# Queries and keys of two head groups projected at once, and spread to padded tiles by transfers

## The chip, the cores and the metric

The kernel runs on one core of one Trainium2 chip. The metric is the device time of one execution in microseconds; the median of three runs of the kernel before is 4207.95 us (4204.61 to 4209.77).

## The reference, cut to what matters

Two layers of a "macaron" block follow each other: a mixture of experts, an attention and a mixture of experts again; then a recurrence, an attention with rotary and relative positions and causal mask, and the recurrence again. Tokens: two sequences of 2048, 256 features, float32. The change concerns the two attentions, 16 heads of 16 features each.

```python
# layer 0                                # layer 1
q = x @ Wq.T * (1 / sqrt(D))             q = shape(x @ w_q.T)
k = x @ Wk.T                             k = shape(x @ w_k.T)
v = x @ Wv.T                             v = shape(x @ w_v.T)
                                         q = _apply_rotary_interleave(q, cos, sin) / 4
                                         k = _apply_rotary_interleave(k, cos, sin)
scores = einsum(q, k)                    scores = einsum(q, k) + einsum(q, rel)
attn = softmax(scores)                   attn = softmax(where(causal, scores, -1e18))
out = (attn @ v) @ Wff.T + bff           out = (attn @ v + einsum(attn, rel)) @ w_o.T
x = x + out                              x = x + out
```

`x` in these lines is the layer-normalised input of the attention; `rel` is an embedding of the clipped distance of query and key.

## The kernel before, in words

The features of the normalised input lie on the partitions (`xnT`, two halves of 128), 512 tokens at a time. The 16 heads are treated in four groups `g` of four heads `j`. A head has only 16 features, but TensorE's row tiles have 32 partitions; so the weights of queries and keys are laid out by `heads` (L1390) with 16 columns of weights and 16 of zeros for each head, and one projection (`mm2`, L135, line L138: two matmuls over the two halves of the features) gives 128 rows: four heads at partitions 0, 32, 64 and 96, each with 16 rows of data and 16 of padding. Row 16 of each padded head has a job: in the keys it holds 1 (added from `krow`, L53, as a bias), and in the queries it takes minus the largest score of each query (`subtract`, L573), so that the score matmul itself subtracts the maximum before the exponential.

**Attention 0** (`attention0`, L641) goes over 32 groups `t` = (sequence `b`, block of 512 queries `qc`, head group `g`). Steps are numbered, eight to a group (`PER`). A step has two halves `n`; in each half TensorE computes four score tiles for the exponentials of an earlier group (`exponential`, L691: 128 keys by 512 queries for each of four heads) and four for the maxima of the present group (`largest`, L678), then the side jobs due at this step, and then the weighted sums of the half-step before (`weighted`, L701). ScalarE turns scores into exponentials (L699), VectorE takes maxima (L686), ScalarE copies the weighted sums out of PSUM (L590), and GpSimd adds them up (L592). Side jobs are put into a table `jobs` with the step at which they are due (`at`): `keys` (L658, ScalarE adds `krow` as it copies, L663), `vals`, `queries` (L670, one for each group, due at step PER*t - 1, copied by ScalarE at L675), `subtract`, `divide`, `outputs_T`, `outputs`. Before the first step, at step -1, eight key projections of the first sequence are made; eight more follow in steps 3 to 6. `pT`, the exponentials, has 12 buffers; keys have 5, queries 3.

**Attention 1** (`attention1`, L898) is causal, so groups with different `qc` have different numbers of key blocks. Its 32 groups are in the order: `qc` 1 for all `g`; then `qc` 2 and `qc` 0 in turn for each `g`; then `qc` 3. A planner (L1153 to L1169) gives each group the steps of its maxima (`Ms` to `Me`), of its exponentials (`Es` to `Ee`), of its positions (`Rs`) and the earliest step `By` of its relative scores; `early` (L1179) is the step of its query projection. `rotate` (L927) makes queries and keys: projection (L931), copy by ScalarE (L933), a shuffle that swaps neighbouring partitions by VectorE (L935), two multiplications with the tables of cosines and sines, the bias for keys and an addition (L937 to L941) by GpSimd, or by VectorE before step 0. `by_position` (L962) multiplies queries with the relative embedding, writes the result through DRAM in a skewed layout and reads it back as `band` (L977, L984); `largest` adds the band, and stores it for `positions_load` (L1053, L1130). The tiles named "s2" serve `rotate`, `by_position`, `positions_load` and `positions_T`; there are four buffers for all. Two tables hold the buffers of queries (4) and keys (12).

TensorE, ScalarE and VectorE issue their instructions in the order in which the program writes them (`manual_schedule`, L1308). The order on GpSimd and on SP, which issues the transfers, is set by the compiling framework's scheduler. An instruction waits at the head of its queue until its operands and its output buffer are free; the ones behind it wait with it. The weights of a later stage take the memory of an earlier one, and their loads wait for its last reader.

Of the kernel before, what the change touches and what calls it, by code (L numbers as in the profile page):

```python
# [10 lines left out]
F32 = mybir.dt.float32  # L11
# [21 lines left out]
G = 4  # L33
# [9 lines left out]
def macaron_kernel(ctx: ExitStack, tc: tile.TileContext, t: dict, out: bass.AP):  # L43
# [9 lines left out]
    krow = const.tile([P, 1], F32, name="krow")  # L53


# [6 lines left out]
    nc.sync.dma_start(out=krow, in_=t["krow"])  # L62
# [69 lines left out]
    def rows(j):  # L132
        return slice(32 * j, 32 * j + 32)

# [376 lines left out]

    HV = H // 2
    VW = DH + 1

    class Pieces:
# [3 lines left out]
        def __init__(self, s, name, norm, weights_o, bias):  # L519
# [4 lines left out]
            for n in range(2):  # L524
                m = self.keep.tile([P, CPB, J, 32], F32, name=f"mneg{n}")
                nc.gpsimd.memset(m, 0.0)
                self.mnegs.append(m)
            self.cn, self.cT, self.o, self.pTs, self.q = ({} for _ in range(5))

# [111 lines left out]
    def attention0(norm, tail, wq, wk_, wv, wo, bff):  # L641
# [7 lines left out]
        with ExitStack() as s:  # L649
            z = Pieces(s, "a0", norm, wo, bff)  # L650
# [6 lines left out]

            def keys(b, g, qc):  # L658
                if qc == 0:
                    kT[b, g] = kpool.tile([P, S], F32, name="kT", bufs=5)  # L660
                pk = bank()
                mm2(pk, wk_[:, :, g], slice(None), z.xnT(b, qc))
                nc.scalar.activation(kT[b, g][:, ts(qc, TB)], pk, AF.Identity, bias=krow)  # L663
# [6 lines left out]
            def queries(t):  # L670
                b, qc, g = groups[t]
                pq = bank()
                mm2(pq, wq[:, :, g], slice(None), z.xnT(b, qc))
                q[t] = wk.tile([P, TB], F32, name="q", bufs=3)
                nc.scalar.activation(q[t], pq, AF.Copy, scale=1.0 / 16.0)  # L675
                mx[t] = wk.tile([P, CPB * J, SB], F32, name="mx")
# [14 lines left out]
            def exponential(t, kb, j):  # L691
# [6 lines left out]
                z.pTs[t, kb, j] = wk.tile([P, TB], F32, name="pT", bufs=12)  # L698
# [18 lines left out]
            for b in range(B):  # L717
# [9 lines left out]
                for g in range(G):  # L727
                    for qc in range(SB):
                        due = first - 6 + PER * g + qc
                        at(due if b else (-1 if g < 2 else 2 * g - 1 + qc // 2), keys, b, g, qc)  # L730
# [4 lines left out]
            for t, (b, qc, g) in enumerate(groups):  # L735
                at(PER * t - 1, queries, t)
# [161 lines left out]
    def attention1(norm, tail, w, relk, relv, kbias, dramp, skew):  # L898
# [4 lines left out]
        with ExitStack() as s:  # L903
            z = Pieces(s, "a1", norm, w["o"], None)
            wk, q = z.wk, z.q
            groups = []
            for b in range(B):
                groups += [(b, 1, g) for g in range(G)]
                groups += [(b, qc, g) for g in range(G) for qc in (2, 0)]
# [17 lines left out]
            def rotate(dst, wa, b, qc, bias):  # L927
# [3 lines left out]
                mm2(pa, wa, slice(None), z.xnT(b, qc))  # L931
# [5 lines left out]
                e.tensor_tensor(dst, xa, cos[b, qc], ALU.mult)  # L937
# [3 lines left out]
                e.tensor_tensor(dst, dst, xb, ALU.add)  # L941

            def keys(b, qc, g):
                if qc:
                    kT[b, qc, g] = wk.tile([P, TB], F32, name="kT", bufs=12)
                elif g % 2 == 0:
                    pair = features_slot()
                    for i in range(2):
                        kT[b, qc, g + i] = pair[:, i, :]
                rotate(kT[b, qc, g], w["k"][:, :, g], b, qc, kbias)  # L950
# [5 lines left out]
            def queries(t):  # L956
                b, qc, g = groups[t]
                q[t] = wk.tile([P, TB], F32, name="q", bufs=4)
                rotate(q[t], w["q"][:, :, g], b, qc, None)
                mx[t] = wk.tile([P, CPB, J, MX], F32, name="mx")  # L960
# [193 lines left out]
            for n, (b, qc, g) in enumerate(groups):  # L1154
# [4 lines left out]
                if n > 3:  # L1159
                    start = max(start, Ee[n - 4] + 2)  # L1160
# [10 lines left out]
            for n, (b, qc, g) in enumerate(groups):  # L1171
# [7 lines left out]
            early = [  # L1179
                max(Ms[n] - 6, Ee[n - 4] + 1) if n > 3 else Ms[n] - 6 for n in range(NG)  # L1180
            ]
            for n in range(NG):
                at(Me[n] + 1, z.subtract, n)
            for n in range(NG):
                at(early[n], queries, n)
            for b in range(B):
                for qc in range(SB):
# [3 lines left out]
                    free = early[index[b, done_, G - 1]] if done_ is not None else f - 12  # L1191
# [273 lines left out]
```

## Time and profile before

| what | value |
|---|---|
| median of three runs | 4207.95 us |
| the profiled execution | 4206.7 us |
| its span | 4204.5 us |
| TensorE busy | 4101.3 us (98%) |
| VectorE, ScalarE, GpSimd busy | 65%, 60%, 43% |
| attention 0, from the first key projection to the last output (L624) | 356 to 2133 us |
| attention 1, from its first query projection to its last output (L624) | 2663 to 4014 us |
| TensorE clock granted, mean | 0.988 of full speed |

In the profile's lines, times are microseconds and means of one instruction nanoseconds. PE is TensorE (PEld its weight loads), DVE VectorE, ACT ScalarE, POOL GpSimd, SPq SyncE's queue, from which transfers start. `s<-b,a_q 128*128 128x512` is a matmul into the PSUM tile `s` with weights of 128 by 128 and a moving tile of 128 partitions by 512 columns. A float32 matmul appears as two records. After a bar come busy time and mean, and after another the idle time ahead of the group with what ended it.

### The profile page before, as it was taken

To read this page: it belongs to the slowest core of one execution; us is meant where nothing else is said; L and a number is where in the kernel's file an instruction comes from. 1 tells how busy PE (TensorE), PEld (TensorE's weight loads), DVE (VectorE), ACT (ScalarE), POOL (GpSimd) and SP (SyncE) were. 2 spreads that over 40 slices of the span, in tenths; PEclk is the share of its full clock that TensorE was granted. 3 is DMA by queue.
4 is the path that set the end of the run, shared out by engine and by line. 5 is a ranking of instruction groups with operands and counts; after the bars stand their busy time and mean duration, and the time that the engine had idled before them with its cause. 6 is when DMAs were issued, how large, how long until landed. Compare 5 with 4: busy or idle time off the path is not lost.

```text
span 4204.5 us, 77295 instructions
## 1 busy us (share of the span) xinstructions
PE 4101.3 (98%) x28512; PEld 1966.6 (47%) x28512; DVE 2720.4 (65%) x6190; ACT 2542.8 (60%) x5155; POOL 1804.3 (43%) x1651
## 2 busy tenths in 40 slices
PE   7999999999999999999989989999999999999999
PEld 4664433333344333333346645555554455554445
DVE  6245787888766778787743444667677665667533
ACT  2332788888877788888833322365657665666832
POOL 4244233336333333333442340466646865654410
PEclk9999999999999999999999999999999999999999
DMA  7341000000000000000043420235432333431201
GB/s 252 119 126 51 1 1 1 1 1 1 1 1 2 1 1 1 1 1 1 9 151 121 128 76 0 71 84 116 100 65 66 74 81 81 107 86 39 46 22 41
DMA packets 355513, 224.29 MB, mean 53 GB/s; under 512 B 146624, under 2 KB 338496, under 8 KB 355136
## 3 DMA queue, kind: packets, MB, share of 16 engines
q1 hardware_dynamic: 342848, 185.77, 17.2%
q0 software_dynamic: 12288, 33.57, 2.5%
q8 instruction: 227, 3.72, 0.4%
q14 instruction: 150, 1.23, 0.1%
HBM read 114.17 MB, written 105.12 MB: 52 GB/s over the span
## 4 chain that ended last, share of the span: by engine, by line
PE 90%; DVE 4%; POOL 3%; issue 1%; DMA 1%; ACT 1%; SPq 0%; POOLq 0%; ACTq 0%; DVEq 0%
PE s L694 13%; PE s L138 12%; PE s L706 12%; PE s L682 10%; PE s L1121 6%; PE s L368 6%; PE s L1007 6%; PE s L1092 6%; PE s L387 3%; PE s L624 1%; PE s L559 1%; PE s L1102 1%; PE s L1106 1%; PE s L1085 1%; PE s L850 1%
## 5 line engine op out<-in xcount | busy, mean ns | idle before, releaser
L592 POOL TENSOR_TENSOR o<-o,part 128x512 f32<-128x512 f32 (+3 forms) x800 | 964.5, 1206 | 1354.2 <-ACT part L590 1350.4
L686 DVE TENSOR_REDUCE mx<-s 128x1 f32<-128x512 f32 x2048 | 1270.3, 682 | 351.6 <-PE s L682 351.4
L699 ACT ACTIVATE pT<-s 128x512 f32<-128x512 f32 x2048 | 1063.5, 617 | 196.3 <-PE s L682 195.4
L682 PE MATMUL s<-kT,q 32*128 32x512 f32 x4096 | 1015.2, 620 | 10.2 <-DVE mx L686 8.9
L694 PE MATMUL s<-q,kT 32*128 32x512 f32 x4096 | 1011.3, 614 | 0.0
L1113 ACT ACTIVATE pT<-s 128x512 f32<-128x512 f32 (+3 forms) x1280 | 589.0, 541 | 224.3 <-PE s L1092 94.7
L694 PEld LDWEIGHTS s<-q,kT 32*128 32x128 f32 x4096 | 414.1, 183 | 462.9 <-DVE mx L686 307.7
L590 ACT COPY part<-s 128x512 f32<-128x512 f32 (+3 forms) x800 | 466.6, 584 | 228.4 <-PE s L1121 115.6
L1015 DVE TENSOR_REDUCE mx<-s 128x1 f32<-128x512 f32 (+1 forms) x768 | 472.7, 678 | 177.7 <-PE s L1007 169.8
L706 PE MATMUL s<-pT,v 128*32 128x512 f32 x4096 | 549.9, 605 | 0.4
L682 PEld LDWEIGHTS s<-kT,q 32*128 32x128 f32 x4096 | 410.7, 184 | 139.4 <-ACT pT L699 73.1
L1007 PE MATMUL s<-kT,q 32*128 32x512 f32 (+7 forms) x2240 | 329.1, 433 | 0.3 <-DVE mx L1036 0.3
L1121 PE MATMUL s<-pT,v 128*32 128x512 f32 (+3 forms) x2560 | 303.8, 542 | 1.1 <-DVE mx L1036 0.8
L368 PE MATMUL s<-we,xT 128*128 x592 | 278.9, 593 | 1.1 <-ACT xT L363 1.1
L375 DVE TENSOR_TENSOR h<-sg,s 128x256 f32<-128x256 f32 x148 | 62.3, 421 | 294.8 <-ACT sg L373 293.3
L1031 DVE CUSTOM_DVE_ANT_0 band<-s,band 128x160 f32<-128x160 f32 (+1 forms) x512 | 155.6, 316 | 129.9 <-PE s L1007 66.3
L706 PEld LDWEIGHTS s<-pT,v 128*32 128x32 f32 x4096 | 82.1, 108 | 335.3 <-ACT pT L699 281.5
L1007 PE MATMUL s<-b,q 32*128 32x512 f32 (+7 forms) x1280 | 234.8, 509 | 3.5 <-DVE b L941 3.3
L1092 PE MATMUL s<-q,kT 32*128 32x512 f32 (+3 forms) x1152 | 237.4, 508 | 0.0
L415 POOL DMA_INDIRECT yg<-results,at x128 | 124.7, 974 | 239.9 <-DMA results<-y 111.3
L1092 PE MATMUL s<-q,b 32*128 32x512 f32 (+3 forms) x896 | 211.0, 569 | 0.1
L1045 POOL TENSOR_TENSOR band<-band,mneg 128x640 f32<-128x640 f32 x128 | 161.5, 1264 | 88.8 <-DVE mneg L1041 88.6
(216 smaller groups left out, 5506.2 us busy)
## 6 DMA issues: line engine op xcount, KB each, us to landing
band<-skew SPq DMA_DIRECT2D x32, 1280.0 KB, 6.2
pd<-band SPq DMA_DIRECT2D x32, 1280.0 KB, 8.1
xs<-places SPq DMA_DIRECT2D x148, 128.0 KB, 2.1
results<-y SPq DMA_DIRECT2D x148, 128.0 KB, 2.0
places<-zero SPq DMA_DIRECT2D x2, 4736.0 KB
we<-in_we SPq DMA_DIRECT2D x12, 768.0 KB, 8.9
skew<-s SPq DMA_DIRECT2D x32, 256.0 KB, 3.0
s<-pd SPq DMA_DIRECT2D x32, 256.0 KB, 7.0
```

The lines of the kernel that those rows point to most:

```text
L138: nc.tensor.matmul(ps, lhsT=w[:, kc, cols], rhs=rhs[:, kc, :], start=start and kc == 0, stop=stop and kc == 1,)
L368: nc.tensor.matmul(pu, lhsT=xT[i][:, ts(kc, P)], rhs=w[:, kc, ds(val[i], 2 * D)], start=kc == 0, stop=kc == 1,)
L592: nc.gpsimd.tensor_tensor(o, o, part[:, q0:], ALU.add)
L682: nc.tensor.matmul(ps, lhsT=q[t][rows(j), ts(qb, P)], rhs=kT[b, g][rows(j), ts(kc, TB)], start=True, stop=True,)
L686: nc.vector.tensor_reduce(mx[t][:, qb * J + j, kc : kc + 1], ps, AX.X, ALU.max)
L694: nc.tensor.matmul(st, lhsT=kT[b, g][rows(j), ts(kb, P)], rhs=q[t][rows(j), :], start=True, stop=True,)
L699: nc.scalar.activation(z.pTs[t, kb, j], st, AF.Exp)
L706: nc.tensor.matmul(pv[rows(j), :], lhsT=v[b, g // 2][:, kb, ds(h * VW, 32)], rhs=z.pTs.pop((t, kb, j)), start=True, stop=True,)
L1007: nc.tensor.matmul(ps[:, ds(cols, n)], lhsT=lhsT, rhs=kT[b, c, g][rows(j), ds(k0, n)], start=True, stop=True,)
L1092: nc.tensor.matmul(ps[:, q0:], lhsT=k, rhs=q[t][rows(j), q0:], start=True, stop=True, skip_group_check=True,)
L1113: nc.scalar.activation(z.pTs[t, kb, j][:, q0:], st.pop((t, kb, j))[:, q0:], AF.Exp)
L1121: nc.tensor.matmul(pv[rows(j), q0:], lhsT=v[b, kb // CPB, g // 2][:, kb % CPB, ds(h * VW, 32)], rhs=z.pTs.pop((t, kb, j))[:, q0:], start=T ...
```

## The change

Queries and keys are projected for two head groups at once: the weights are no longer padded, and one projection gives 128 full rows, 8 heads of 16 features. ScalarE (attention 0) or `rotate` (attention 1) leaves them in a packed tile, and `spread` brings each group of four heads to its padded tile with four transfers of 16 partitions by 512 columns, one for each head. The padding is now written separately. Query tiles are fixed (4 in attention 0, 6 in attention 1), and GpSimd clears the two of a pair before they are filled. Key tiles are fixed too, and `pad_keys` writes their padding (1 in row 16, 0 below) by four transfers, once for each fixed tile, and for the keys of block 0 in attention 1 each time. `krow` is gone. The queries of a pair are due one step earlier in attention 0, and keys two steps earlier in attention 1; in attention 0 all keys of the first sequence come at step -1. In attention 1 the groups of `qc` 2 and `qc` 0 go in pairs of head groups. `pT` in attention 0 has 8 buffers, `mx` 4; the first two value projections of attention 1 move to step -2.

```diff
+    def spread(dst, src, i):
+        for j in range(J):
+            nc.sync.dma_start(
+                out=dst[32 * j : 32 * j + DH], in_=src[ds(64 * i + DH * j, DH), :]
+            )
+
+    def pad_keys(dst):
+        n = dst.shape[-1]
+        for j in range(J):
+            nc.sync.dma_start(out=dst[32 * j + DH : 32 * j + 32], in_=t["pads"][j, :, 0:n])
...
+            self.qs = [
+                self.keep.tile([P, TB], F32, name=f"q{n}") for n in range(queries)
+            ]
...
+        def clear_queries(self, t):
+            for i in range(2):
+                self.q[t + i] = self.qs[(t + i) % len(self.qs)]
+                nc.gpsimd.memset(self.q[t + i], 0.0)
...
+            keep_k = [kpool.tile([P, S], F32, name=f"kT{n}") for n in range(5)]
+            padded = set()
             def keys(b, g, qc):
-                if qc == 0:
-                    kT[b, g] = kpool.tile([P, S], F32, name="kT", bufs=5)
+                for i in range(2):
+                    n = (b * G + g + i) % 5
+                    kT[b, g + i] = keep_k[n]
+                    if (n, qc) not in padded:
+                        padded.add((n, qc))
+                        pad_keys(keep_k[n][:, ts(qc, TB)])
                 pk = bank()
-                mm2(pk, wk_[:, :, g], slice(None), z.xnT(b, qc))
-                nc.scalar.activation(kT[b, g][:, ts(qc, TB)], pk, AF.Identity, bias=krow)
+                mm2(pk, wk_, ts(g // 2, P), z.xnT(b, qc))
+                packed = wk.tile([P, TB], F32, name="packed")
+                nc.scalar.copy(packed, pk)
+                for i in range(2):
+                    spread(kT[b, g + i][:, ts(qc, TB)], packed, i)
...
             def queries(t):
                 b, qc, g = groups[t]
+                z.clear_queries(t)
                 pq = bank()
-                mm2(pq, wq[:, :, g], slice(None), z.xnT(b, qc))
-                q[t] = wk.tile([P, TB], F32, name="q", bufs=3)
-                nc.scalar.activation(q[t], pq, AF.Copy, scale=1.0 / 16.0)
-                mx[t] = wk.tile([P, CPB * J, SB], F32, name="mx")
+                mm2(pq, wq, ts(g // 2, P), z.xnT(b, qc))
+                packed = wk.tile([P, TB], F32, name="packed")
+                nc.scalar.activation(packed, pq, AF.Copy, scale=1.0 / 16.0)
+                for i in range(2):
+                    spread(q[t + i], packed, i)
+                    mx[t + i] = wk.tile([P, CPB * J, SB], F32, name="mx", bufs=4)
...
-                z.pTs[t, kb, j] = wk.tile([P, TB], F32, name="pT", bufs=12)
+                z.pTs[t, kb, j] = wk.tile([P, TB], F32, name="pT", bufs=8)
...
-                for g in range(G):
+                for g in range(0, G, 2):
                     for qc in range(SB):
-                        due = first - 6 + PER * g + qc
-                        at(due if b else (-1 if g < 2 else 2 * g - 1 + qc // 2), keys, b, g, qc)
+                        at(first - 7 + PER * g + qc if b else -1, keys, b, g, qc)
...
-                at(PER * t - 1, queries, t)
+                if t % 2 == 0:
+                    at(PER * t - 2, queries, t)
...
-                groups += [(b, qc, g) for g in range(G) for qc in (2, 0)]
+                for g in range(0, G, 2):
+                    groups += [(b, qc, g + i) for qc in (2, 0) for i in range(2)]
...
-            def rotate(dst, wa, b, qc, bias):
+            def rotate(wa, b, qc, g, bias):
                 pa = bank()
-                mm2(pa, wa, slice(None), z.xnT(b, qc))
+                mm2(pa, wa, ts(g // 2, P), z.xnT(b, qc))
...
-                e.tensor_tensor(dst, xa, cos[b, qc], ALU.mult)
+                e.tensor_tensor(xa, xa, cos[b, qc], ALU.mult)
...
-                e.tensor_tensor(dst, dst, xb, ALU.add)
+                e.tensor_tensor(xa, xa, xb, ALU.add)
+                return xa
+
+            keep_k, packed = {}, {}
+            for qc in range(1, SB):
+                for g in range(G):
+                    keep_k[qc, g] = z.keep.tile([P, TB], F32, name=f"kT{qc}{g}")
+                    pad_keys(keep_k[qc, g])
...
+                for i in range(2):
+                    k = kT[b, qc, g + i] = keep_k[qc, g + i] if qc else pair[:, i, :]
+                    if qc == 0:
+                        pad_keys(k)
+                packed[b, qc, g] = rotate(w["k"], b, qc, g, kbias)
+
+            def keys_out(b, qc, g, i):
+                spread(kT[b, qc, g + i], packed[b, qc, g], i)
...
+                z.clear_queries(t)
+                xa = rotate(w["q"], b, qc, g, None)
+                for i in range(2):
+                    spread(q[t + i], xa, i)
+                    mx[t + i] = wk.tile([P, CPB, J, MX], F32, name="mx", bufs=2)
...
-                if n > 3:
-                    start = max(start, Ee[n - 4] + 2)
+                if n > 5 and n % 2 == 0:
+                    start = max(start, Ee[n - 5] + 4)
...
-                max(Ms[n] - 6, Ee[n - 4] + 1) if n > 3 else Ms[n] - 6 for n in range(NG)
-            ]
+                n: max(Ms[n] - 6, Ee[n - 5] + 1) if n > 5 else Ms[n] - 6 for n in range(0, NG, 2)
+            }
...
-                        at(f - 4 + (qc == 0), keys, b, qc, g)
+                        at(f - 6 + (qc == 0), keys, b, qc, g)
+                        for i in range(2):
+                            last_ = Ee[index[b - 1, SB - 1, g + i]] if b and qc else -99
+                            at(max(f - 6 + (qc == 0), last_ + 1), keys_out, b, qc, g, i)
...
-                        at(Es[index[b, max(qc, 1), 2 * half]] - 1 + (qc == 0), vals, b, qc, half)
+                        due = Es[index[b, max(qc, 1), 2 * half]] - 1 + (qc == 0)
+                        at(due if b or qc > 1 or half else -2, vals, b, qc, half)
...
-                at(max(By[n], early[n] + 1), by_position, n)
+                at(max(By[n], early[n - n % 2] + 2), by_position, n)
```

## The prediction, made before the changed kernel was run

> **What bounds the kernel now.** I read the page's busy shares and slices first, then the chain that ended last, then stages, then the timeline of single half-steps.
>
> ```profile
> PE 4101.3 (98%) x28512; PEld 1966.6 (47%) x28512; DVE 2720.4 (65%) x6190; ACT 2542.8 (60%) x5155; POOL 1804.3 (43%) x1651
> ...
> PE 90%; DVE 4%; POOL 3%; issue 1%; DMA 1%; ACT 1%; SPq 0%; POOLq 0%; ACTq 0%; DVEq 0%
> ```
>
> TensorE is busy for 98% of the span and is 90% of the chain; the next engine has 65%. A busy TensorE may hide waiting, so I look at one half-step of attention 0 without and one with a projection (timeline, TensorE only: start, length, line, count).
>
> ```profile
> 995.45 0.69 PE L694 MATMUL s<-q,kT 32*128 32x512 f32 x1
> ...
> 997.38 1.98 PE L138 MATMUL s<-b,a_q 128*128 128x512 f32 x4
> 999.30 1.06 PE L706 MATMUL s<-pT,v 128*32 128x512 f32 x8
> 1000.29 0.69 PE L694 MATMUL s<-q,kT 32*128 32x512 f32 x1
> ...
> 1005.74 1.07 PE L706 MATMUL s<-pT,v 128*32 128x512 f32 x8
> ...
> 1008.66 1.06 PE L706 MATMUL s<-pT,v 128*32 128x512 f32 x8
> ```
>
> A plain half-step recurs every 2.92 us (L706, the last operation in it, at 1005.74 and 1008.66): four waves of scores and two of weighted sums at 0.43 us are 2.57, and 0.35 is the change of tile shapes. ScalarE needs 2.06 + 0.59 and VectorE 2.46 in it, both less. With a projection the half-step takes 4.84 (995.45 to 1000.29): the projection costs 1.92, all of it on the path. Check: attention 0 from 432 to 2133 is 1701 us; 512 half-steps of 2.92 are 1495, and the side jobs are the rest. So TensorE is dense there. Attention 1 is alike:
>
> ```profile
> 2707.00:4014.00 1307.00, 1286.33 (x11370) 670.95 (x11368) 863.99 (x2574) 839.39 (x1782) 798.15 (x705) 0.99 0.36 79
> ```
>
> TensorE (first number) is busy 98% of this stage; a key projection there lasts 1.82 (2774.28 to 2776.10). The work to be halved (groups by form; records, two to a matmul):
>
> ```profile
> L138 PE MATMUL s<-b,a_k 128*128 128x512 f32 x256 | 128.8, 633 | 0.8 <-DVE mx L1015 0.5
> L138 PE MATMUL s<-b,a_q 128*128 128x512 f32 x256 | 127.5, 621 | 4.6 <-DVE mx L1031 4.4
> ```
>
> 512 records, four to a projection: 128 projections, 32 for keys and 32 for queries in each attention.
>
> **What the Trainium skill says.** "TensorE: Matmul & The Clock Gate", "Why this matters for your kernels": a matmul with a short contraction takes as long as a full one; streamed columns set the time. So a packed projection of two groups costs what a padded one of one group costs; the trace agrees: all L138 records have a median of 592 ns. "TensorEngine Tiling (Array Packing)", "Key Properties": changing the tiling mode drains the engine; 1.92 against 4 x 0.43 = 1.72 agrees. "DMA: Bandwidth & Descriptors", "Rules for kernel authors": under 64 KB a transfer is mostly overhead; a spread moves 32 KB. No small SBUF-to-SBUF transfer is in this trace; the nearest rows are below. "SBUF — State Buffer", "Who interferes with whom": transfers don't contend with compute engines; I price spreads by issue and latency alone, and no run here isolates that.
>
> **The change, part by part.**
>
> (1) *Attention 0, projections.* 32 + 32 become 16 + 16. Of the 16 queries that go, 15 lie in dense half-steps: 15 x 1.92 = 28.8. Of the key projections 8 go in batch 1: 8 x 1.92 = 15.4. The other 8 went in the ramp (396 to 420), where VectorE's four maxima take 2.72 per half-step against 2.98 with a projection: 8 x 0.26, with 0.9 where two fell together and 0.3 for a query, 3.3. Sum 47.5.
>
> (2) *Attention 1, projections.* Again 32 go. Three (second query and two keys) were in the ramp, 29 x 1.82 = 53. The planner's rules, worked through for the new group order, give 170 steps as before, so no steps are won or lost. GpSimd loses about half the rotation (60 rotations at 3.8 to 5.4 us become 29), VectorE 32 shuffles (0.74), ScalarE 64 copies: nothing on the path, TensorE being dense.
>
> (3) *Spreads and pads.* 512 spreads and 160 pads are issued by SP. Prices:
>
> ```profile
> xs<-places SPq DMA_DIRECT2D x148, 128.0 KB, 2.1
> skew<-s SPq DMA_DIRECT2D x32, 256.0 KB, 3.0
> ```
> ```profile
> 2448.07 0.44 SPq L129 DMA_DIRECT2D a_k<-in_a_k  x1
> 2448.57 0.42 SPq L129 DMA_DIRECT2D a_v<-in_a_v  x1
> 2449.03 0.43 SPq L129 DMA_DIRECT2D a_o<-in_a_o  x1
> ```
>
> Issues back to back are 0.47 apart, whatever the size (bounds: 0.32, the shortest issue, and 0.50, the 32 fills of L1295 in 15.6 us); landing 2.1 (1.9 to 3.0). Not below zero: a transfer is only added. Eight spreads take 3.8, and the last lands 5.9 us after the data.
> In attention 0's steady part a query is projected two steps ahead: some 9.7 us (rest of its step and 5.84) against 0.6 for the copy, 1.9 for the first tile's four issues and 2.1: covered. Two "packed" buffers are each held some 6.5 us and used at most once a step: covered. The 32 query clears (0.53, the price of L526) lie on GpSimd, 0.4 busy: covered. pT with 8 buffers instead of 12 is free: the weighted sums that release a set precede, on TensorE, the scores that need it.
>
> (4) *Start of attention 0.* All eight pair projections of batch 0 come before the first scores, each with 8 spreads and, the first time, 8 pads. Cover: VectorE is in L420 until 382.5 (TensorE waits from 374.4 to 383.26 as it is), having the expert results fetched by GpSimd one per 1.25 us. kT0's pads must wait for the shared weights under it (last read at 356); the other tiles' I expect in SP's idle time after 336. Then 16 pads from 356 end at 363.5, the query's and the first six keys' spreads (56 x 0.47) at 390, landing at 392. The eighth key's copy needs the sixth's buffer, and the eighth score needs the bank of the eighth key: VectorE ends those two half-steps at some 396 instead of 387.5. Loss 8; bounds 0 (pads early) and 25 (48 more pads in the way, or the query clear behind GpSimd's fetches until 380).
>
> (5) *Start of attention 1.* Pads for 12 key tiles lie first in order; those over the recurrence's last buffers are freed about 2666, and 32 x 0.47 = 15 us of pads precede the query's spreads (data at 2669). Two value projections (2 x 1.9) move into the waiting. Loss 10; bounds 0 and 20.
>
> (6) *Attention 1, waits that arise.* The rotated tile takes one of four "s2" buffers, now held 5.9 us longer, and query and keys of a pair often fall in the same step. Behind the waiting shuffle on VectorE are the maxima, and behind those TensorE's banks. Laying out who holds which buffer, with steps of 7.4 us (1307 over some 165 steps is 7.9) and rotations of 6.5 to 9.5 (from each projection to L941's end), I count seven waits of 3 to 5 us for shuffles, 29 in all against 7 before (one wait of 3.26 at L935 is there now). About half reaches TensorE: 12; bounds 0 and 40. SP is in order too, and much blocked:
>
> ```profile
> SPq L1053 <- POOL band L1045: 377.3, 32, 46.4
> SPq L984 <- DMA skew<-s: 92.8, 31, 7.4
> ```
>
> A spread behind such a wait is mostly covered: after rotation a query has some 20 us before L970 reads it (9 at worst before the change, once past the start; by the new rules never under three steps from its projection). The band's own chain gets spreads in its way: 5; bounds 0 and 25.
>
> **Sum.** Gain 47.5 + 53 = 100.5; losses 8 + 10 + 12 + 5 = 35; net 65. The profiled execution took 4206.7 (span 4204.5 and 2.2 around it): 4206.7 - 65 = 4142; its median is 1.3 higher: 4143.
>
> **Rivals.** *All covered*: the losses stay near 4; 100.5 - 4 = 96, 4111. For it: GpSimd and SP have idle time, slack is 20 us. Against it: the starts, where nothing covers.
> *Attention 1 gives its gain back*: losses there of some 60 instead of 27, net 32: 4176. For it: four buffers and an in-order SP.
> *Slower*: one mechanism, in attention 1: each of the 32 pair rotations makes the next user of an s2 buffer, on in-order VectorE or ScalarE, wait for the spreads to land, and TensorE with it. Without parts of (6) the net is 82, so it decides from 82/32 = 2.6 us a rotation; the full hold is 5.9. At 4 us: 128 - 82 = +46, 4254. Against it: average use of the four buffers falls (160 allocations for 224).
> *The change doesn't do what it says*: excluded for the projections, whose number is in the loops.
>
> **Chances.** Likeliest (4115 to 4160) 0.45; covered (below 4115) 0.17; given back (4160 to 4199) 0.15; within 0.2%, which is about what a measurement of this kernel can tell from no change, 0.04; slower 0.19. Range 4098 to 4220: it leaves out the lowest covered cases and most of the slower ones.
>
> **What would show it.** Right: 256 fewer L138 records, about 28,256 on TensorE; plain half-steps still 2.92; attention 0 (356 to 2133) shorter by some 40, attention 1 (2663 to 4014) by some 26; TensorE idle at both starts. Wrong: VectorE's shuffle or ScalarE's copies waiting on DMA through attention 1; scores waiting for q or kT by DMA in the steady part; half-steps longer than 2.92.

## The result, and the profile after

The changed kernel takes 4237.81 us (median of four runs, 4234.78 to 4241.61) against 4208.49 for the kernel before on the same chip: ratio 1.0072, 95% interval 1.0054 to 1.0089. It is slower by 0.7%, where 4143 and "faster" were forecast. The profiled execution has a span of 4237.5 us.

The page of the changed kernel, first busy times and shares, then the chain that ended last:

```profile
PE 4045.4 (95%) x28256; PEld 1952.4 (46%) x28256; DVE 2696.1 (64%) x6122; ACT 2499.4 (59%) x5091; POOL 1696.8 (40%) x1606
...
PE 24%; POOL 2%; issue 2%; DVE 2%; DMA 2%; ACT 1%; SPq 0%; POOLq 0%; ACTq 0%; DVEq 0%
```

TensorE lost 256 records and 56 us of busy time, and still the kernel is longer: its share fell from 98 to 95%. The chain accounts for only a third of the span this time, so it isn't read further. The stages tell more (stretch, its length, then busy time of PE, PEld, DVE, ACT, POOL, the clock granted to PE, the DMA share, GB/s): attention 0, then MoE 2 with the first recurrence, then attention 1.

```profile
357.30:2087.80 1730.50, 1712.75 (x13178) 656.63 (x13177) 1360.25 (x2292) 1359.44 (x2639) 682.27 (x597) 0.99 0.04 11
2087.80:2617.70 529.90, 506.50 (x1817) 299.44 (x1816) 229.32 (x603) 152.35 (x341) 155.62 (x177) 0.98 0.29 92
2617.70:4046.30 1428.60, 1312.02 (x11425) 690.39 (x11424) 877.72 (x2613) 828.58 (x1763) 695.77 (x653) 0.95 0.40 83
```

Before, the same stages took 1776.3, 531.0 and 1349.7. So attention 0 gained 45.8 us, the middle stayed, and attention 1 lost 79. Attention 0 is as dense as before; its plain half-steps, read from one weighted sum to the next without a projection between them, are still 2.92 us (timeline, TensorE):

```profile
987.53 1.07 PE L740 MATMUL s<-pT,v 128*32 128x512 f32 x8
...
990.45 1.07 PE L740 MATMUL s<-pT,v 128*32 128x512 f32 x8
```

The projections are halved, 128 records each for 256 (minimum, median and maximum in ns):

```profile
L146 PE MATMUL s<-b,a_q x128: 592/592/697, 357.3 to 3826.3; 128*128 128x512 f32 x128
L146 PE MATMUL s<-b,a_k x128: 592/592/1221, 359.0 to 3828.0; 128*128 128x512 f32 x128
```

In attention 1 TensorE stands idle for 117 us (26 before), and the mean clock is 0.95 in place of 0.99. I split the stage with windows of 5 us: idle time, and of the busy time the part that the granted clock took away (busy x (1 - clock)); the rest is work at full clock.

| kernel | attention 1, us | idle | lost to a slow clock | work at full clock |
|---|---|---|---|---|
| before | 1350.0 | 26 | 10 | 1314 |
| after | 1428.9 | 117 | 43 | 1269 |

Work fell by 45, idle time rose by 90, the slow clock took 34 more: 90 + 34 - 45 = 79. So the projections were saved, and given back nearly three times over as waiting.

One wait of many, followed back. SP (start, time from the start of the first issue to the end of the last, line, transfer, count):

```profile
2730.03 5.71 SPq L134 DMA_DIRECT2D q<-s  x8
2736.65 4.93 SPq L134 DMA_DIRECT2D kT<-s  x8
2741.68 0.53 SPq L1178 DMA_DIRECT2D s<-pd  x1
```

ScalarE, which needs that last transfer, and TensorE behind it:

```profile
2745.53 0.63 ACT L1186 ACTIVATE s<-s 128x512 f32<-128x512 f32 x1 [11.88 <-DMA s<-pd]
```

```profile
2746.69 1.46 PE L1154 MATMUL s<-ident,band 128*128 128x128 f32 x4 [9.04 <-ACT part L609]
```

The load of the positions (`positions_load`, s<-pd) stands on SP behind sixteen spreads, which can be issued only as GpSimd's rotations end. ScalarE reaches the exponential of the positions and stands 11.88 us; everything behind it on ScalarE stands too, among it the copies (L609) that free TensorE's banks, and TensorE loses 9.04. And that isn't all (windows of 5 us over the same place; the column before the last two is the clock):

```profile
2735.00:2740.00 5.00, 2.65 (x24) 1.05 (x18) 3.05 (x14) 0.00 (x0) 4.92 (x5) 0.98 0.18 39
2740.00:2745.00 5.00, 0.00 (x0) 0.00 (x0) 0.00 (x0) 0.00 (x0) 0.01 (x1) 0.50 0.48 81
2745.00:2750.00 5.00, 3.29 (x18) 2.05 (x20) 0.00 (x0) 3.33 (x7) 2.27 (x3) 0.50 0.00 0
2750.00:2755.00 5.00, 5.00 (x36) 3.86 (x31) 3.13 (x5) 2.17 (x4) 1.47 (x2) 0.66 0.67 149
2755.00:2760.00 5.00, 4.82 (x38) 1.85 (x37) 3.34 (x6) 1.49 (x6) 1.27 (x1) 1.00 0.66 113
```

After the gap TensorE is busy again from 2746.69 but runs at half clock until some 2753. The gap of 9.0 us costs about 12.

SP's own waits, those shown of before and the new one:

```profile
SPq L1101 <- POOL band L1093: 304.8, 27, 45.8
...
SPq L134 <- POOL s L976: 166.0, 26, 28.8
...
SPq L1032 <- DMA skew<-s: 100.3, 31, 5.7
```

SP waits 166 us at spreads for GpSimd's rotations; what is late is what is queued behind.

### The profile page after: what moved, and what is told of

Read it like the earlier page. It is cut to its first block, busy times and chain, and to the rows that moved or that the text cites. A ratio compares the mean times of both kernels' runs of the same rounds, so it can differ in the third digit from the quotient of the medians.

```text
span 4237.5 us, 78186 instructions
## 1 busy us (share of the span) xinstructions
PE 4045.4 (95%) x28256; PEld 1952.4 (46%) x28256; DVE 2696.1 (64%) x6122; ACT 2499.4 (59%) x5091; POOL 1696.8 (40%) x1606
## 5 line engine op out<-in xcount | busy, mean ns | idle before, releaser
L716 PE MATMUL s<-kT,q 32*128 32x512 f32 x4096 | 1030.3, 623 | 11.2 <-DVE mx L720 10.4
L609 ACT COPY part<-s 128x512 f32<-128x512 f32 (+3 forms) x800 | 467.3, 585 | 277.4 <-PE s L1169 160.4
L1055 PE MATMUL s<-kT,q 32*128 32x160 f32 (+7 forms) x2240 | 339.9, 441 | 22.9 <-ACT part L609 21.5
L1169 PE MATMUL s<-pT,v 128*32 128x512 f32 (+3 forms) x2560 | 313.6, 558 | 22.8 <-DVE mx L1079 13.2
L1055 PE MATMUL s<-b,q 32*128 32x512 f32 (+7 forms) x1280 | 244.3, 520 | 3.5 <-ACT part L609 2.0
```

What stands on the lines that cost most here:

```text
L609: nc.scalar.copy(part[:, q0:], pv[:, q0:])
L716: nc.tensor.matmul(ps, lhsT=q[t][rows(j), ts(qb, P)], rhs=kT[b, g][rows(j), ts(kc, TB)], start=True, stop=True,)
L1055: nc.tensor.matmul(ps[:, ds(cols, n)], lhsT=lhsT, rhs=kT[b, c, g][rows(j), ds(k0, n)], start=True, stop=True,)
L1169: nc.tensor.matmul(pv[rows(j), q0:], lhsT=v[b, kb // CPB, g // 2][:, kb % CPB, ds(h * VW, 32)], rhs=z.pTs.pop((t, kb, j))[:, q0:], start=T ...
```

## The experiments

Theories: **(Q)** SP's in-order queue: spreads stand ahead of other transfers that are due, above all the load of the positions. **(P)** the pairs of causal groups: two narrow groups (qc = 0) in a row get their bands late. **(B)** the four s2 buffers, held until spreads land. **(S)** the start of attention 1: pads and spreads before anything can run. The kernels ran in five groups. In three of them the kernel before takes 4206 to 4208 us; in two (e5 to e8, e9 to e12) it takes 4296 to 4297, with the loss in other stages. There I compare ratios and the length of attention 1. One kernel was run on both (e11, e18) and gave 0.9938 and 0.9909, and 1354.1 and 1363.7 us of attention 1, so that differences under 0.003 or 10 us between the two are not read. Attention 1 of all kernels, in the manner of the table above:

| kernel | attention 1, us | idle | slow clock | work |
|---|---|---|---|---|
| e1 attention 0 alone | 1350.4 | 26 | 11 | 1314 |
| e2 order alone | 1378.9 | 53 | 11 | 1315 |
| e5 order, fill on VectorE | 1350.7 | 28 | 8 | 1315 |
| e3 positions on ScalarE's queue | 1391.8 | 84 | 37 | 1270 |
| e4 late pads | 1418.7 | 107 | 43 | 1268 |
| e6 order 2, 0, 2, 0 | 1396.3 | 92 | 36 | 1268 |
| e7 e6 + e3 | 1386.9 | 80 | 33 | 1274 |
| e8 e7 + e4 | 1384.6 | 74 | 36 | 1274 |
| e9 e8, one s2 user less | 1373.6 | 67 | 33 | 1273 |
| e12 e3, fill on VectorE | 1360.2 | 70 | 18 | 1271 |
| e13 four edits | 1368.1 | 66 | 32 | 1270 |
| e17 e13, first pads early | 1347.1 | 58 | 19 | 1270 |
| e10, e11 keys alone packed | 1360.8, 1354.1 | 49, 50 | 24, 12 | 1288, 1292 |
| e14, e18 keys alone | 1381.4, 1363.7 | 56, 50 | 30, 24 | 1295, 1290 |

**Which attention, and which part of the change.** e1 is the kernel before with the new `attention0`, `spread`, `pad_keys` and weights; `attention1` is untouched.

> Attention 0 packed and spread as in the kernel after, attention 1 as in the kernel before. If the 45.8 us by which attention 0 became shorter stand for themselves and all of the loss lies in attention 1: 4208 - 46 = 4162, 4155 to 4170. If part of the loss comes from elsewhere (for instance a lower granted clock later on[...]): 4175 to 4210.

4162.09 us, ratio 0.9902 (0.9886 to 0.9919). As the first theory said, to the microsecond: attention 0 gives 45, and all of the loss lies in attention 1. Its stage (columns as above) is that of before:

```profile
2617.30:3967.70 1350.40, 1324.67 (x11553) 690.14 (x11551) 902.40 (x2681) 846.67 (x1795) 821.45 (x741) 0.99 0.37 80
```

e2 is the kernel before with only the order of groups:

```diff
-                groups += [(b, qc, g) for g in range(G) for qc in (2, 0)]
+                for g in range(0, G, 2):
+                    groups += [(b, qc, g + i) for qc in (2, 0) for i in range(2)]
```

> The kernel before with one line of the change: the causal groups of attention 1 in the order 2, 2, 0, 0 in place of 2, 0, 2, 0. Theory of the pairs (two narrow groups one after the other bring their bands through memory too late): VectorE's and GpSimd's waits for the band rise as in the kernel after, 15 to 40 us slower, 4225 to 4250. Theory of SP's queue (transfers of the spread stand ahead of the band and of the positions): nothing of this is in this kernel, within 8 us of 4208.

4234.92 us, ratio 1.0072 (1.0055 to 1.0089): 28 us for one line, with no spread in the attention. Theory P, then, and at the size expected. Where it goes (timeline of e2, first GpSimd, then TensorE):

```profile
2911.21 0.20 POOL L1029 MEMSET band<- 128x128 f32 x1 [11.19 <-DMA band<-skew]
...
2922.81 1.26 POOL L592 TENSOR_TENSOR o<-o,part 128x512 f32<-128x512 f32 x1
```

```profile
2924.12 1.11 PE L601 MATMUL s<-ident,o 128*128 128x128 f32 x4 [10.94 <-POOL o L592]
```

The fill of the band's first columns (0.20 us of work) waits 11.19 us on GpSimd for the band of the second narrow group. Then GpSimd works through what has gathered behind it, 1.26 us each, among it the sum (L592) that TensorE's transpose needs: 10.94 us of TensorE.

e3 is the kernel after with one word changed:

```diff
             def positions_load(t):
...
-                nc.sync.dma_start(
+                nc.scalar.dma_start(
```

> The kernel after, but the load of the positions (s from pd) is issued on ScalarE's queue, so it no longer stands on SP behind spreads that wait for GpSimd. Theory of SP's queue: the five PE gaps behind ScalarE's exponential of the positions (9.0, 5.3, 5.4, 7.2 and 3.4 us, 30 in all) go and some of the lost clock with them, 4195 to 4210. Rival, the band is the cause and these gaps only change their name: 4230 to 4245. Rival, ScalarE now waits itself for pd to be written: 4240 to 4270.

4201.16 us, ratio 0.9985 (0.9978 to 0.9992): 37 us under the kernel after, in the middle of what theory Q gave. At the place shown above the load no longer queues, and ScalarE hardly waits:

```profile
2731.04 0.38 ACTq L1178 DMA_DIRECT2D s<-pd  x1
...
2734.94 0.63 ACT L1186 ACTIVATE s<-s 128x512 f32<-128x512 f32 x1 [0.32 <-DMA s<-pd]
```

The Trainium skill ("DMA: Bandwidth & Descriptors", "Issuing engines are not separate DMA queues") says that issuing from several engines saves only the time of issuing, which is small. Here the issues of one line, 32 of 0.38 us, were moved, and 37 us went, since an issue also waits for all that stands ahead of it on its engine.

e4 is the kernel after with the pads of each kept tile moved from the start into `keys`, at its first use:

```diff
                     keep_k[qc, g] = z.keep.tile([P, TB], F32, name=f"kT{qc}{g}")
-                    pad_keys(keep_k[qc, g])
...
-                    if qc == 0:
+                    if qc == 0 or b == 0:
                         pad_keys(k)
```

> The kernel after, but each kept key tile of attention 1 gets its pads where it is first used, so that the 48 pad transfers (29.5 us on SP) no longer stand ahead of the cosines at the start of attention 1. Theory of the start: the gap of 17 us at 2623 goes and the stage starts 15 to 19 us earlier, 4217 to 4223. Rival, the start waits for the spreads anyway, and the pads cost the same later: 4230 to 4245.

4231.35 us, ratio 1.0066 (1.005 to 1.0083): 6 us of the 15 to 19 expected. The first weighted sums come 63.9 us after the first projection instead of 72.3 (52.9 before). So the pads ahead of the stage were 8.4 of the 19.4 us that the start lost; what is left is not taken apart by this run. The wait itself is in one piece in the kernel after, and ends when the first spread queries land (TensorE):

```profile
2640.01 2.05 PE L1018 MATMUL s<-relk,q 128*128 128x128 f32 x8 [16.96 <-DMA q<-s]
```

**The order's mechanism, and the order in the changed kernel.** e5 is e2 with the fill on VectorE, which waits for the band right after anyway:

```diff
-                            nc.gpsimd.memset(band[t][:, 0, :, 0:BAND], MASKED)
+                            nc.vector.memset(band[t][:, 0, :, 0:BAND], MASKED)
```

> The kernel before with the causal groups in pairs (4234.9 in the run of that alone), and the small fill of the band's first columns, which waits for the band to arrive, given to VectorE in place of GpSimd. Theory: the 28 us of the order are GpSimd standing at that fill while the transposes of outputs wait for its sums; they go, 4203 to 4215. Rival, the band of the second narrow group is itself too late for VectorE and PE: 4225 to 4240.

4297.52 us, ratio 1.0002 (0.9993 to 1.0011). All 28 us are gone with the order kept: the cost was GpSimd standing at the fill, not the band's being late for the scores.

e6 is the kernel after with the order 2, 0, 2, 0; `queries(t)` fills the tiles of t and of the group after the next, and the plan's buffer rule follows.

```diff
+                groups += [(b, qc, g) for g in range(G) for qc in (2, 0)]
...
-                for i in range(2):
-                    spread(q[t + i], xa, i)
+                for i, m in enumerate((t, other[t])):
+                    spread(q[m], xa, i)
```

> The kernel after with the causal groups back in the order 2, 0, 2, 0; queries are still projected and rotated two head groups at once, one for this group and one for the group after the next. Theory of the pairs: the 28 us that the order alone cost come back, 4203 to 4215. Theory of SP's queue: the waits behind the spreads stay and take most of it, 4225 to 4240.

4303.99 us, ratio 1.0017 (1.0011 to 1.0024), attention 1 32 us shorter. The 28 us come back in the changed kernel too, as theory P said (the ratio, 0.0055 under the kernel after, makes it 24).

e7 adds e3's edit to it, e8 adds e4's.

> The same order 2, 0, 2, 0, and also the load of the positions on ScalarE's queue. If the two causes are separate, their gains add: 4238 - 37 - 28 = 4173, 4165 to 4180. If they share waits: 4185 to 4205. Under 4162 (attention 0 alone changed), packing pays in attention 1 too.

4295.80 us, ratio 1.0000 (0.9991 to 1.0009). A miss: the two gains don't add. Attention 1 is 9 us shorter than in e6, not 37.

> The same as the last, and each kept key tile gets its pads where it is first used. The late pads alone were worth 6 us (8 at the start of the stage, some of it given back): 4159 to 4175 if that holds here too; no less than the last run if what is left at the start is the wait for the spread of queries.

4292.35 us, ratio 0.9994 (0.9985 to 1.0003). A miss again: the pads are worth 3 us here, not to be told from none. The trace of e8 shows one reason: on ScalarE's queue ScalarE itself stands until the load can be issued (first SP, then ScalarE).

```profile
3002.45 6.29 SPq L134 DMA_DIRECT2D q<-s  x8
```

```profile
3008.44 0.39 ACTq L1184 DMA_DIRECT2D s<-pd  x1
3008.93 0.48 ACT L609 COPY part<-s 128x384 f32<-128x384 f32 x1 [8.97 <-DMA q<-s]
```

It is not an s2 buffer that this load waits for. The eight spreads read one buffer, and the load leaves at 3008.44, while SP is still issuing the last of them (until 3008.74); in the trace's semaphore records only the first has landed by then, at 3008.37, and the other seven land from 3008.54 to 3010.28. The same records show what it waits for: the transfers signal their landing on eight semaphores in turn, whether SP or ScalarE issues them, and the load has that of the first spread. In e7, e8, e9, e13, e14 and e17 loads on ScalarE's queue stand for 3.9 to 8.7 us nine times, and each leaves within 0.2 us of the landing of the transfer just before it on its own semaphore. In five of the nine that one is a pad, which touches nothing of the load's. This is read from the traces; no run changes the semaphores.

e9 takes one user out of the s2 buffers:

```diff
-                wT[t] = wk.tile([P, TB], F32, name="s2", bufs=4)
+                wT[t] = wk.tile([P, TB], F32, name="part", bufs=3)
```

> The last kernel (order 2, 0, 2, 0; positions loaded on ScalarE's queue; late pads; ratio 0.9994 to the kernel before) with the copy of the transposed positions taken out of the four s2 buffers and put into the three part buffers, so that one of five users of s2 is gone. Theory of the s2 buffers (a rotated tile holds its buffer until its eight spreads have landed, and the load of the positions, now on ScalarE's queue, stands until one is free): the waits of 9 and 3.4 us go, ratio 0.995 to 0.9975. Rival, the buffers are not what it waits for: 0.9985 to 1.0005.

4285.21 us, ratio 0.9964 (0.9951 to 0.9977): 11 us less in attention 1 than e8. Two gaps of 3.4 us of TensorE behind the copy of the transposed positions are gone; the one of 7.1 us behind the load (at 3002 in e8) stays with 6.9, as it must if no buffer is behind it. The copy before one of the two gaps (e8, VectorE):

```profile
3099.18 0.69 DVE L1199 COPY s<-s 128x512 f32<-128x512 f32 x1 [3.61 <-POOL s L980]
```

It waits for the buffer until GpSimd ends a rotation (L980), not until spreads land. So theory B holds with about 11 us and not more, and for these waits not in the form that it had.

e12 leaves the pairs, and has e3's edit and e5's:

> The kernel after, pairs and pads as they are, with two edits: the load of the positions on ScalarE's queue and the fill of the band's first columns on VectorE. If the two waits are separate, 37 and 26 us: 4238 - 63 = 4175, ratio 0.990 to 0.9945. If they are one wait with two names: 4195 to 4205, ratio 0.997 to 0.9995.

4271.38 us, ratio 0.9945 (0.9928 to 0.9961), attention 1 68.7 us shorter than after. The ratio is at the edge of what two separate waits gave, and the stage's length (37 + 29 = 66 expected from e3 and e2) fits them within the 10 us named above: Q and P are two causes, and together they are most of the 79 (of the 124 us that waiting and slow clock took in all, some 55%).

**Keys alone.** e10 packs only the keys in attention 1; queries, order and plan are those of before, pads late.

```diff
+                q[t] = wk.tile([P, TB], F32, name="q", bufs=4)
+                rotate(w["q"][:, :, g], b, qc, slice(None), None, q[t])
```

> Attention 0 as in the kernel after; in attention 1 only the keys are packed and spread, the queries are projected and rotated per head group as in the kernel before, with its order and its plan; late pads. If the spreads of the queries, which are due soon, are what costs: keys alone gain their share, 16 fewer key projections of 1.8 us less some at the start, 4162 - 29 + 10 = 4143, ratio 0.982 to 0.988. If any spread that waits for GpSimd in front of the band and the positions costs: half of the loss, 4162 + 15, ratio 0.990 to 0.998.

4270.37 us, ratio 0.9935 (0.9918 to 0.9952): within the range of the second. Packing the keys alone costs more than the 26 us of work that it saves; one gap alone is 14 us (TensorE behind ScalarE behind s<-pd, at 2790). That the spreads are the cause is not shown: between the last spreads and this load SP issues 19 pads, which this run places late (SP):

```profile
2781.49 8.50 SPq L141 DMA_DIRECT2D kT<-in_pads  x16
...
2796.36 0.43 SPq L1175 DMA_DIRECT2D s<-pd  x1
```

> The same with five s2 buffers in place of four. Theory of the s2 buffers: 5 to 15 us faster than with four (ratio lower by 0.001 to 0.0035). Rival: within 4 us of it.

With `bufs=5` for s2: 4269.44 us, ratio 0.9938 (0.9922 to 0.9955), no difference. Here the buffers aren't what is waited for.

**What the rest is.** e13 is the kernel after with the edits of e3, e5, e4 and e9.

> The kernel after with four edits: positions loaded on ScalarE's queue, the band's fill on VectorE (together 0.9945), each key tile's pads at its first use, the transposed positions in the part buffers. If the rest of the loss is at the start and in the s2 buffers: 8 us and 10 to 13 us less than with the first two, ratio 0.989 to 0.991. If the spreads as such hold the stage up: within 6 us of 0.9945.

4170.86 us, ratio 0.9911 (0.9898 to 0.9925), just above the range of the first theory. Attention 1 still takes 18 us more than before, with 44 us less work. By the stage's length it is no better than e12 (1368.1 against 1360.2), though its ratio is 0.0034 lower, so what the two further edits gave is not shown.

> Attention 0 packed; in attention 1 only the keys, five s2 buffers, late pads (0.9938), and now the positions loaded on ScalarE's queue. If what is left of the loss is the load of the positions behind the spreads of keys (one gap of 14 us, one of 3.4, and the slow clock behind them): 15 to 20 us less, ratio 0.989 to 0.9905. If the spreads of keys as such cost: within 5 us of 0.9938.

Keys alone with the load on ScalarE's queue: 4192.24 us, ratio 0.9961 (0.9948 to 0.9975). A miss, to the wrong side. As in e8 the load waits for a transfer on its own semaphore, now a pad that lands at 2692.03, and holds ScalarE twice over:

```profile
2692.20 0.38 ACTq L1175 DMA_DIRECT2D s<-pd  x1
2692.63 0.48 ACT L609 COPY part<-s 128x384 f32<-128x384 f32 x1 [8.77 <-DMA kT<-in_pads]
2701.93 0.63 ACT L1183 ACTIVATE s<-s 128x512 f32<-128x512 f32 x1 [7.70 <-DMA s<-pd]
```

e15 is e13 with the first pair's query spreads issued by ScalarE:

```diff
-                    spread(q[t + i], xa, i)
+                    spread(q[t + i], xa, i, nc.scalar if step < 0 else nc.sync)
```

> The four edits, and the first pair of query spreads, eight transfers, is issued on ScalarE's queue, so that SP has the keys' alone. If the start waits for the issue of these transfers one after another (8 of 0.62 us): 3 to 6 us less than with the four edits. If the first gap is VectorE's rotation: within 2 us of them.

4179.41 us, ratio 0.9927 (0.9914 to 0.9941): no gain; a loss is not shown, as the intervals overlap and attention 1 takes 1368.1 us in both profiles. ScalarE has to copy the keys out of the bank next, and that copy now stands behind the spreads:

```profile
2627.47 5.11 ACTq L134 DMA_DIRECT2D q<-s  x8
2632.63 1.07 ACT L968 COPY s<-s 128x512 f32<-128x512 f32 x2 [9.71 <-DMA q<-s]
```

> Attention 0 packed, attention 1 as before, once more on the same chip as these: 45 us under the kernel before, ratio 0.989 to 0.991. If packing pays in attention 1 once its waits are gone, the others end under it; if not, at it or over it.

4162.41 us, ratio 0.9889 (0.9874 to 0.9904), as e1.

e17 is e13 with the pads of qc = 1 back at the start and the others at first use:

```diff
+                    if qc == 1:
+                        pad_keys(keep_k[qc, g])
...
-                    if qc == 0 or b == 0:
+                    if qc == 0 or (b == 0 and qc > 1):
```

> The four edits (ratio 0.9911), but the 16 pads of the four tiles that the first groups read are issued ahead of the stage (10 us on SP, before the cosines are due), and only the other 32 at first use. If the pads among the first spreads hold the start up: 4 to 8 us less, 4163 to 4167, ratio 0.989 to 0.9905. If the start is VectorE's rotation and the spreads themselves: within 3 us of 4171.

4160.07 us, ratio 0.9898 (0.9883 to 0.9913), 11 us under e13, more than the 4 to 8 expected; but the ratios are 5 us apart and their intervals overlap, so the size is loose. The table's two profiles make it look larger: e13's execution was 5.4 us above its median, e17's 3.5 below. The first weighted sum comes 59.7 us after the first projection, in e13 63.8. The start, from SP's timeline, first of the kernel after and then of e17:

```profile
2599.29 29.46 SPq L141 DMA_DIRECT2D kT<-in_pads  x48
2628.79 0.42 SPq L960 DMA_DIRECT2D cos<-in_cos  x1
...
2636.04 5.00 SPq L134 DMA_DIRECT2D q<-s  x8
```

```profile
2598.49 13.43 SPq L141 DMA_DIRECT2D kT<-in_pads  x16
2616.17 0.35 SPq L960 DMA_DIRECT2D cos<-in_cos  x1
...
2623.65 5.29 SPq L134 DMA_DIRECT2D q<-s  x8
```

With 16 pads the cosines leave 12.6 us earlier and so do the queries' spreads. Attention 1 of e17:

```profile
2616.90:3964.00 1347.10, 1289.10 (x11425) 683.22 (x11424) 878.57 (x2621) 826.68 (x1763) 694.06 (x645) 0.98 0.39 88
```

> Keys alone packed in attention 1, five s2 buffers, late pads, positions on SP; this was 0.9938 on another chip. If the load on ScalarE's queue (0.9961) made it worse, this is at 4176 to 4186; if the two chips differ in what the transfers cost, it is near 4192 too.

4170.47 us, ratio 0.9909 (0.9896 to 0.9923). So for keys alone the load on ScalarE's queue costs 22 us (e14), where with queries and keys packed it gains 37 (e3): it depends on what the load waits for in its new place. In e3 no load holds ScalarE for more than 2.5 us, in e14 one does for 8.3 and another for 6.2.

The best versions are e1 (4162, attention 0 alone) and e17 (4160, all packed, five edits), not to be told apart. Packing in attention 1, with its waits mended, is worth nothing that can be measured: 44 us of work saved, 32 back as idle time, 10 as slow clock.

## Why the prediction was wrong, step by step

- **(1) Attention 0's projections, gain 47.5, and (4) its start, loss 8.** Right: 45.8 measured, 39.5 forecast. In the manner of the table, work fell by 51 us, a little more than priced; idle time rose by 1 and the slow clock by 5, in place of the 8 lost at the start (TensorE resumes at 384.94 where it resumed at 383.26).
- **(2) Attention 1's projections, gain 53.** Right in kind, a little too large: 45 us of work at full clock. A packed projection costs what a padded one does (592 ns a record in both), though not by the rule that was cited: the zeros lie in the columns of the weights, and the contraction is over 128 partitions before and after. That the plan keeps its number of steps is no proof that the order of groups is free: the order alone costs 28 us (e2), and the step priced it at nothing.
- **(3) Price of a spread, 0.47 us, at most 0.50.** Mis-sized for the spreads: eight take 5.00, 0.62 each. The price was taken from loads into all 128 partitions and not from a transfer of this kind, which the trace before didn't have; the upper bound should have been wider. For the pads it holds: in the kernel after they follow each other at 0.46 to 0.47, and the 29.46 us of the 48 contain two waits of SP, 6.3 and 1.3 us. The landing (2.1, at least 1.9) holds too: the fourth spread of the first query tile is issued at 2637.92 and lands at 2639.87, and TensorE reads the tile at 2640.01.
- **(5) Start of attention 1, loss 10, at most 20.** Mis-sized: 19.4 (72.3 against 52.9 to the first weighted sum). The step put only the 32 late pads ahead of the spreads. All 48 stood ahead of the cosines, which the rotation needs first; with 16 ahead of them (e17) the start lost 6.9.
- **(6) Waits in attention 1, 12 for s2 buffers and 5 for the band's chain.** This is the step that failed. It asked when a spread itself is needed, found 20 us of slack, and called it covered. The spreads were covered: after the start no wait of a computing engine ends with the landing of a spread in attention 1 of the kernel after. It named SP as in order, but asked of each queue only whether the spread is late, not what stands behind the spread. The load of the positions stood behind it (37 us, e3), and it was not among the transfers priced. The band's chain was priced at 5 (at most 25) for spreads in its way; what counted was the order, which made GpSimd stand at a fill (28 us, e2 and e5). The s2 buffers, on which the step spent its working, are about 11 us where they could be told apart (e8 to e9). That this is near the 12 given is luck in part: VectorE's shuffles do wait for GpSimd's rotations much as counted (24.7 us in five waits, 29 in seven forecast), but the 11 us came from another user of the buffers, the copy of the transposed positions.
- **The sum left out a term.** A gap of TensorE was counted at its length. Of the 124 us that attention 1 gave back (79 + 45), 34 are the slow clock behind the gaps. "TensorE: Matmul & The Clock Gate", "Part 1: The HAM clock gate", in the Trainium skill says so: after an idle window of some 3.4 us the clock is halved, and a busy window restores it. The windows of 0.50 above agree, and so do the clock records of the kernel after: its stage has 17 stretches at half clock (5 before), each of 3.41 us or a small multiple of it, and each takes 1.6 to 4.7 us, 2.7 on average.
- **The rivals.** "Slower" came true with another mechanism. Its price was each rotation's making the next user of an s2 buffer wait for the spreads to land; no such wait of VectorE or ScalarE is in the trace, and e9 and e11, which ease the buffers, gave 11 us and nothing. The in-order SP stands only as a word for "gives its gain back" (4176); it deserved a rival and a price of its own. The signs listed for being wrong were those of the s2 mechanism, and none of them came: VectorE's shuffles and ScalarE's copies in `rotate` wait on transfers for 0.2 us in all, and after the start no scores wait for q or kT.

What stays open: with five edits attention 1 is idle 58 us against 26. Some 14 of this are three gaps at the start, the last of them (3.8) behind a load that waits for a pad on its semaphore, and two of 2 to 3 us wait for a band to come back from DRAM; the rest is in many short gaps that no run took apart. A fifth s2 buffer with all packed was not run, nor a single transfer per tile in place of four, nor the load on a queue and semaphore of its own.

## What to carry to other kernels

When transfers are added to a queue, list what is issued behind each of them, and when that is due: a spread with 20 us of slack of its own held up a load with none. Do the same for every in-order engine that is made to wait on a transfer, even for a fill of 0.2 us. Moving a transfer to another engine's queue moves its waits there as well: one such move gained 37 us in one kernel here and cost 22 in another. Read in the trace which landing ends such a wait; here it was often one that the load had no use for. On a TensorE as dense as this one, price a gap at its length and some 2 to 3 us of half clock behind it (2.7 on average in the kernel after); many short gaps are dearer than one long one.

## What the runs showed of the hardware beyond that

- Gaps shorter than 3.4 us halve the clock as well, which the skill's window does not lead one to expect: in e13 a gap of 2.43 us at 3009 is followed by a window at 0.50 (3015 to 3020), and in the kernel before one of 3.24 at 3490 by 0.58. In e2 gaps of 10.9, 5.2 and 13.3 us cost hardly more clock than short ones do: TensorE was back at 1.00 less than 6 us after the first of them, and the clock took 2.7, 2.4 and 2.1 us of work there, against 4.8 after the gap of 2.43 in e13.
- The kernel before took 4206 to 4208 us on three chips and 4296 to 4297 on two. The difference isn't in attention 1 (1350.0 us in the kernel before on one of the first, 1350.7 in e5 on one of the second); in the first 340 us, which are alike in e2 and e5, TensorE was busy for 317 us at a clock of 0.98 in e2 and for 289 at 0.93 in e5.
